# Per-tile reuse of the convolution's room, and constants made by GpSimd alone, in a convolution and attention hybrid

## The chip, the cores and the metric

The kernel runs on one core of a Trainium2 chip. A core has five engines with queues of their own: TensorE (PE in the profile, with PEld for its weight loads), VectorE (DVE), ScalarE (ACT), GpSimd (POOL) and SyncE (SP), which here only issues DMAs. Each takes its instructions in order. They meet through semaphores: an instruction can wait until a count that other instructions raise has reached a value. The metric is the device time of one execution in microseconds; lower is better. Before the change it is 2581.11 us, the median of five runs between 2576.23 and 2585.54.

## The reference

The input x has 128 images of 128 channels and 16x16 pixels. The model has two layers.

```
# layer 0
x = x + conv_block(group_norm(x))
#   conv_block: batch norm, 4-bit activations, 3x3 conv (4-bit weights, cross pattern),
#               batch norm, 4-bit activations, 3x3 conv (diagonal pattern), + its input
# layer 1, tokens t = pixels of x
t = t + mamba(ln(t), forward weights) + reversed mamba(ln(t), backward weights)
t = t + moe(ln(t))          # 8 experts, the best 2 of them, softmax of their scores
```

The batch norm of the convolution block has to see all images before any of them can go on, so layer 0 has three passes: statistics, the first convolution, the second convolution. Layer 1 treats each image by itself.

## The kernel before

Images are handled in 64 pairs. A pair is a tile of 128 channels by 512 pixels in float32, 256 KB, or 2 KB in each of the 128 partitions of the on-chip memory.

**Statistics and first convolution.** All 64 pairs of x are loaded into tiles xr0 to xr63 (lines 374 to 378), which stay on chip to the end of the second convolution. They live in the pool `res` with the second convolution's weights `wq2`, four padded images `hpad` and small tensors. The first convolution writes its output to DRAM (o1), apart from five pairs kept on chip.

**Second convolution** (`conv2`, lines 546 to 601). For each pair: the first convolution's output comes back from DRAM (q), ScalarE applies batch norm and Relu (L562), VectorE quantises into a padded image (L195), TensorE convolves (L222), GpSimd and at times ScalarE scale xr in place (L592, L590), VectorE adds (L593), TensorE transposes the result to tokens (L571), ScalarE copies it out of PSUM (L573), and SP stores it to DRAM as y (L574). GpSimd's scaling depends on little, so it runs far ahead of the other engines. Which taps and how many passes the convolution needs is decided on the chip: `by_weights` reads a flag and branches to one of three versions of the phase, so the code of the second convolution stands three times in the program, inside If blocks.

**The room.** When the convolution is done, `ress.close()` and `kepts.close()` release its pools, and the pools of the loop take over the same memory: `late` (constants), `pr` and `sm` (working tiles), `ps` (PSUM). A pool that lands on released pools waits, as written, for every user of those pools. So the first instruction that writes into `late` waits for the last use of anything in `res`.

**Constants** (`constants`, lines 619 to 639, with the memsets of line 646). `rows` and `cols` are three sets each of bf16 operands, 4 KB per partition, for a matmul that makes the decay matrices (part s, L933). A set of rows is filled by one ScalarE copy (a column repeated along the free axis, L623) and overwritten in its first 64 partitions by a VectorE copy of repeated identities (L624); a set of cols by a VectorE copy (L628) and eight GpSimd masks (L635). `gts`, `daz`, `lwz` and `far` are set by GpSimd memsets (L646, L620).

**The loop.** Layer 1 is written as small generators, the parts: a (load a pair of tokens, layer norm, transpose), c (time steps and decays, once per two pairs), x, z, s, y and so on, to f (experts and output). A part yields after each step. The table `T` gives every step a time, with 375 units for each two pairs; all steps of all pairs are sorted by it and issued in that order under `manual_schedule`, so it is the order on each engine. Part a of pair 0 has its steps at 60 (load yt0 from y, L712), 68 (statistics on VectorE, L693 to L696), 103 (the power -1/2 and two products on GpSimd, L699 to L701), 165 (normalize on ScalarE, L704), 270 (transpose on TensorE, L718) and 336 (copy from PSUM, L721); pair 1 has them at 191, 257, 313, 327, 385 and 395. Part c of these two pairs follows from 420 with the matmuls dt_ps (L734), which need both. `constants()` is called just before the steps. All DMAs before the change are issued by SP.

Of the kernel before, what the change touches and what calls it, by code (L numbers as in the profile page):

```python
# [8 lines left out]
F32 = mybir.dt.float32  # L9
# [5 lines left out]
P = 128  # L15
NT = 256
# [6 lines left out]
NH = 4  # L23
HD = 64
# [10 lines left out]
def kernel(ctx: ExitStack, tc: tile.TileContext, a: dict):  # L35

    nc = tc.nc
    x_d, out_d = a["x"], a["out"]
    B = x_d.shape[0]
    NP = B // 2  # L40
    NG = B // G
    PSUM = bass.MemoryType.PSUM

    x_c = x_d.rearrange("b c s -> c b s")
# [6 lines left out]
    y_d = [dram.tile([P, 4, P], F32, name=f"y_{i}", tag=f"y_{i}") for i in range(NP)]  # L51
# [8 lines left out]
    ident = const.tile([P, P], F32, name="ident")  # L60
# [32 lines left out]
    heads = const.tile([P, NH], F32, name="heads")  # L93
    triple = const.tile([P, 2], F32, name="triple")
# [166 lines left out]

    ress = ExitStack()
    res = ress.enter_context(tc.tile_pool(name="res", bufs=1))
    wq2 = res.tile([P, 9, 3, P], BF16, name="wq2")

    hpads = [res.tile([P, 2, 18, 18], F32, name=f"hpad{k}") for k in range(4)]
# [81 lines left out]
    with tc.tile_pool(name="w1p", bufs=1) as w1p:  # L348
# [15 lines left out]
        with tc.tile_pool(name="setup1", bufs=1) as setup, tc.tile_pool(  # L364
            name="psa", bufs=1, space=PSUM
# [5 lines left out]
                next(weights)  # L371


            xr = []
            for i in range(NP):
                t = res.tile([P, 2, NT], F32, name=f"xr{i}", tag=f"xr{i}")
                nc.sync.dma_start(t, x_c[:, 2 * i : 2 * i + 2, :])
                xr.append(t)
            load_weights()
            w2 = w1p.tile([P, 9, P], F32, name="w2", tag="w")  # L380
            nc.sync.dma_start(w2, a["L0_conv_w2"])
# [223 lines left out]
    ress.close()  # L605
    kepts.close()

    late = ctx.enter_context(tc.tile_pool(name="late", bufs=1))

# [7 lines left out]
    def constants():  # L619
        nc.gpsimd.memset(far, -1e30)  # L620
        for k in range(3):
            r, c = rows[k], cols[k]
            nc.scalar.copy(r.rearrange("p h d t l -> p h (d t l)"), heads.unsqueeze(2).to_broadcast([P, NH, 4 * P]))  # L623
            nc.vector.tensor_copy(  # L624
                r[0:HD].rearrange("p h d t (f l) -> p (h d t f) l", l=HD),
                ident[0:HD, 0:HD].unsqueeze(1).to_broadcast([HD, 2 * NH * 2 * 2, HD]),
            )
            nc.vector.tensor_copy(  # L628
                c.rearrange("p m d j f l -> p m (d j f l)"), triple.unsqueeze(2).to_broadcast([P, 2, 8 * P])
            )  # L630
            for d in range(2):
                for half in range(2):
                    sign = 1 - 2 * d
                    for m in range(2):
                        nc.gpsimd.affine_select(  # L635
                            out=c[0:HD, m, d, :, half, :], in_=far.unsqueeze(2).to_broadcast([HD, 2, P]),
                            pattern=[[0, 2], [sign, P]], compare_op=ALU.is_ge, fill=0.0,
                            base=-sign * HD * half - 1, channel_multiplier=-sign,
                        )
# [4 lines left out]
    lwz = late.tile([P, P], F32, name="lwz")  # L644
    for t in (*gts, daz, lwz):
        nc.gpsimd.memset(t, 0.0)  # L646
    pr = ctx.enter_context(tc.tile_pool(name="pr", bufs=2))
    sm = ctx.enter_context(tc.tile_pool(name="sm", bufs=2))
    ps_ = ctx.enter_context(tc.tile_pool(name="ps", bufs=1, space=PSUM))
    BANKS = {"x": 2, "y": 2, "o": 4}  # L650
    E0 = 5

# [3 lines left out]
    def bank4(name, tag):  # L656
        return bank(name, tag).rearrange("p (t l) -> p t l", l=P)
# [29 lines left out]
    def layernorm(src, dst, nm):  # L687

        s6 = sm.tile([P, 4, 6], F32, name=f"s6{nm}", tag="s6")
        mv = sm.tile([P, 4, 2], F32, name=f"mv{nm}", tag="mv")  # L690
        rstd = sm.tile([P, 4], F32, name=f"rstd{nm}", tag="rstd")
        for t in range(4):
            nc.vector.bn_stats(s6[:, t, :], src[:, t, :])  # L693
        for t in range(4):
            nc.vector.bn_aggr(mv[:, t, :], s6[:, t, :])
        alone(nc.vector.tensor_scalar(rstd, mv[:, :, 1], EPS, None, ALU.add))  # L696
        yield
        nmr = sm.tile([P, 4], F32, name=f"nmr{nm}", tag="nmr")
        nc.gpsimd.tensor_tensor(rstd, rstd, mhalf[:, :4], ALU.pow)  # L699
        nc.gpsimd.tensor_tensor(nmr, mv[:, :, 0], rstd, ALU.mult)  # L700
        nc.gpsimd.tensor_scalar(nmr, nmr, -1.0, None, ALU.mult)  # L701
        yield
        for t in range(4):
            nc.scalar.activation(  # L704
                dst[:, t, :], src[:, t, :], AF.Identity, bias=nmr[:, t : t + 1], scale=rstd[:, t : t + 1]
            )
        yield

    def part_a(i):

        yt = yts[i] = pr.tile([P, 4, P], F32, name=f"yt{i}", tag="yt", bufs=6)
        nc.sync.dma_start(yt, y_d[i])  # L712
        yield
        u = pr.tile([P, 4, P], F32, name=f"u{i}", tag="u", bufs=2)
        yield from layernorm(yt, u, f"a{i}")
        u_ps = bank4(f"u_ps{i}", "o")
        for t in range(4):
            nc.tensor.transpose(u_ps[:, t, :], u[:, t, :], ident)  # L718
        yield
        uT = uTs[i] = pr.tile([P, 4 * P], F32, name=f"uT{i}", tag="uT", bufs=4)  # L720
        nc.scalar.copy(uT, u_ps.rearrange("p t l -> p (t l)"))  # L721
        yield
# [425 lines left out]
    def part_f(i):  # L1148
# [83 lines left out]
    }  # L1232
    parts = {
        "a": part_a, "c": part_c, "x": part_x, "bc": part_bc, "sx": part_sx, "z": part_z, "xt": part_xt, "g": part_g,
        "s": part_s, "b": part_b, "m": part_m, "y": part_y, "n": part_n, "r": part_r, "o": part_o, "e": part_e, "p": part_p,
        "f": part_f,
    }
    steps = []
    for i in range(NP):
        for (name, *which), places in T.items():  # L1240
# [3 lines left out]
            steps += [(i // 2 * PERIOD + t, len(steps) + n, stream) for n, t in enumerate(places[i % 2])]  # L1244
    steps.sort(key=lambda step: step[:2])
    constants()
    with tc.manual_schedule():
        for _, _, stream in steps:
# [31 lines left out]
```

## Time and profile before

| | |
|---|---|
| median of five runs | 2581.11 us |
| the profiled execution | 2579.19 us, span 2577.5 us |
| PE, DVE, ACT, POOL busy | 94%, 88%, 85%, 64% of the span |
| second convolution on TensorE | about 175 to 294 us |
| the loop's first TensorE instruction | 312.12 us |
| steady part of the loop | about 420 to 2500 us |

The profile is one execution on the chip. Times are counted from the start of its span; the execution's own time holds 1.7 us more than the span. A line such as "L592 POOL TENSOR_SCALAR xr<-xr,ares,bres 128x256" is a group of instructions: line of the kernel, engine, operation, output and inputs, and the shape of the output; what follows is busy time, the mean of one, and the idle time of the engine just before. In lists by time the first two columns are start and length, x24 means 24 instructions in a row, and square brackets give how long the engine had been idle and what released it. POOLq and SPq are the sequencers that issue and wait for these engines. For the stretches of time, columns are named where they are shown.

### The profile page before, as it was taken

What the parts mean: (1) busy time and instruction counts of PE and PEld (TensorE: products, weight loads), DVE (VectorE), ACT (ScalarE), POOL (GpSimd) and SP (SyncE); (2) the same over time, 40 slices, a digit from 0 to 9 for tenths busy, and PEclk for the clock granted to TensorE, in tenths of its full rate; (3) what the DMA queues carried; (4) which work ended last, traced back from release to release, by engine and by line L of the source; (5) the groups of instructions that cost most, each with busy time, mean ns of one, the idle gap of its engine ahead of it and who ended that gap; (6) DMA issues with size and microseconds to landing.
All of it is one profiled execution on the core that took longest, in us unless ns stands there. A gap on an engine that the chain in (4) does not pass through costs nothing.

```text
span 2577.5 us, 49413 instructions
## 1 busy us (share of the span) xinstructions
PE 2434.4 (94%) x15940; PEld 1483.2 (58%) x15940; DVE 2259.6 (88%) x6193; ACT 2192.6 (85%) x4482; POOL 1656.1 (64%) x1727
## 2 busy tenths in 40 slices
PE   0889679999999999999999999999999999999997
PEld 0335345666666666666666666666666666666663
DVE  8877589999999999999999999999999999999883
ACT  6777579898988889889888898998888898988881
POOL 1777315666667666666676666666666666666666
PEclk9999889999999999999999999999999999999998
DMA  9458423443444444444434444343434444443343
GB/s 284 147 199 280 165 62 90 125 123 118 130 119 118 123 131 131 121 121 123 125 112 123 128 130 119 120 127 122 119 119 131 131 123 118 126 125 114 109 126 104
DMA packets 303030, 339.03 MB, mean 132 GB/s; under 512 B 56865, under 2 KB 226849, under 8 KB 302753
## 3 DMA queue, kind: packets, MB, share of 16 engines
q1 hardware_dynamic: 302752, 335.68, 43.1%
q8 instruction: 132, 2.16, 0.3%
q14 instruction: 146, 1.19, 0.2%
HBM read 261.41 MB, written 57.41 MB: 124 GB/s over the span
## 4 chain that ended last, share of the span: by engine, by line
PE 90%; DVE 3%; DMA 3%; ACT 2%; POOL 1%; issue 1%; SPq 0%; POOLq 0%; DVEq 0%; ACTq 0%
PE f_ps L1157 17%; PE x_ps L845 13%; PE y_ps L980 9%; PE z_ps L888 9%; PE o_ps L1040 9%; PE cv L222 5%; PE sg L933 5%; PE xt_ps L900 4%; PE y_ps L986 4%; PE g_ps L919 4%; DMA xr<-in_x 2%; PE n_ps L1013 1%; PE u_ps L718 1%; PE f_ps L1152 1%; PE u_ps L1062 1%; PE yt_ps L571 1%
## 5 line engine op out<-in xcount | busy, mean ns | idle before, releaser
L1145 POOL TENSOR_TENSOR gb<-gb,u2T 128x512 f32<-128x512 f32 x512 | 641.6, 1278 | 121.5 <-PE y_ps L986 60.2
L863 DVE SCALAR_TENSOR_TENSOR xc<-x_ps,cw,xc 128x510 f32<-128x510 f32 (+2 forms) x768 | 571.2, 744 | 46.6 <-ACT xc L857 37.2
L996 POOL TENSOR_TENSOR yg<-yg,z 128x512 f32<-128x512 f32 x256 | 325.8, 1278 | 352.2 <-DVE yg L992 155.4
L1157 PE MATMUL f_ps<-gb,ew 128*128 128x512 f32 x1024 | 511.7, 604 | 6.0 <-POOL gb L1145 5.8
L845 PE MATMUL x_ps<-uT,wx 128*128 128x512 f32 x768 | 401.9, 605 | 8.5 <-DVE xc L863 3.5
L673 ACT ACTIVATE e<-sg 128x512 f32<-128x512 f32 x512 | 299.5, 591 | 49.9 <-PE sg L933 44.5
L673 ACT ACTIVATE e<-e,ends 128x128 f32<-128x128 f32 x1024 | 325.0, 392 | 0.0
L980 PE MATMUL y_ps<-e,xt 128*64 128x256 f32 x2048 | 317.7, 389 | 0.2 <-DVE yg L992 0.2
L961 DVE TENSOR_TENSOR e<-e,g_ps 128x1024 f32<-128x1024 f32 x256 | 311.4, 1216 | 6.3 <-ACT e L673 2.6
L863 DVE SCALAR_TENSOR_TENSOR bc<-x_ps,cw,bc 128x510 f32<-128x510 f32 (+2 forms) x384 | 286.5, 746 | 20.5 <-ACT bc L857 5.2
L1157 PEld LDWEIGHTS f_ps<-gb,ew 128*128 128x128 f32 x1024 | 181.3, 192 | 173.6 <-issue 137.6
L888 PE MATMUL z_ps<-uT,wz 128*128 128x512 f32 x512 | 271.2, 611 | 2.0 <-DVE xc L863 1.4
L857 ACT ACTIVATE xc<-x_ps,cb,cw 128x512 f32<-128x512 f32 x256 | 199.1, 778 | 64.5 <-PE x_ps L845 57.9
L1040 PE MATMUL o_ps<-wo,yg 128*128 128x128 f32 x2048 | 251.0, 276 | 0.2 <-DVE e L966 0.2
L1040 PEld LDWEIGHTS o_ps<-wo,yg 128*128 128x128 f32 x2048 | 240.3, 193 | 11.1 <-DVE g L1117 8.4
L992 DVE SCALAR_TENSOR_TENSOR yg<-xc,dcol,y_ps 128x512 f32<-128x512 f32 x256 | 189.6, 741 | 50.4 <-PE y_ps L986 46.9
L1028 POOL TENSOR_TENSOR rr<-rr,mhalf 128x8 f32<-128x8 f32 x64 | 109.9, 1717 | 161.4 <-DVE g L1119 82.4
L986 PE MATMUL y_ps<-e,xt 128*64 128x128 f32 x2048 | 198.9, 273 | 0.0
L933 PE MATMUL sg<-rows,cols 128*128 128x256 bf16 x1024 | 192.2, 275 | 5.8 <-ACT e L673 2.8
L222 PE MATMUL cv<-hpad,wq 128*128 128x512 bf16 x640 | 179.1, 423 | 18.0 <-DVE hpad L195 8.8
L986 PEld LDWEIGHTS y_ps<-e,xt 128*64 128x64 f32 x2048 | 146.9, 137 | 74.2 <-DVE e L966 0.5
L980 PEld LDWEIGHTS y_ps<-e,xt 128*64 128x64 f32 x2048 | 118.8, 136 | 101.0 <-issue 53.9
(257 smaller groups left out, 4870.2 us busy)
## 6 DMA issues: line engine op xcount, KB each, us to landing
gb<-gd SPq DMA_DIRECT2D x256, 512.0 KB
e<-cum SPq DMA_DIRECT2D x256, 256.0 KB
xr<-in_x SPq DMA_DIRECT2D x64, 256.0 KB
y<-yt SPq DMA_DIRECT2D x64, 256.0 KB
yt<-y SPq DMA_DIRECT2D x64, 256.0 KB
cc<-bc SPq DMA_DIRECT2D x128, 128.0 KB
out<-ob SPq DMA_DIRECT2D x64, 256.0 KB
o<-o SPq DMA_DIRECT2D x59, 256.0 KB
```

The costliest lines, as they stand in the source:

```text
L673: nc.scalar.activation(out, in_, func, **more)
L845: nc.tensor.matmul(ps, wx[d][:, n * P : (n + 1) * P], uTs[i], start=True, stop=True)
L863: nc.vector.scalar_tensor_tensor(acc[:, :, to], raw[:, :, of], cw[:, d, n, 3 - back : 4 - back], acc[:, :, to], ALU.mult, ALU.add,)
L888: nc.tensor.matmul(ps, wz[:, d, n * P : (n + 1) * P], uTs[i], start=True, stop=True)
L933: nc.tensor.matmul(sg[:, :, of], c_[:, k, d, s, half, :], r_[:, :, d, s, of], start=True, stop=True)
L961: nc.vector.tensor_tensor(e0.rearrange("p h t l -> p h (t l)"), e0.rearrange("p h t l -> p h (t l)"), gps[i, d, k][:, 0:NT].unsqueeze(1).t ...
L980: nc.tensor.matmul(y_ps[64 * q : 64 * q + 64, k, :], xt[:, 2 * k + s0, 64 * h : 64 * h + 64], e0[:, h].rearrange("p t l -> p (t l)"), star ...
L986: nc.tensor.matmul(y_ps[64 * q : 64 * q + 64, k, s1 * P : (s1 + 1) * P], xt[:, 2 * k + s1, 64 * h : 64 * h + 64], e1[:, h, :], start=False ...
L996: large(nc.gpsimd.tensor_tensor(yg, yg, zs[i, d][:, n, :], ALU.mult))
L1040: nc.tensor.matmul(o_ps[:, (2 * j + d) * P : (2 * j + d + 1) * P], ygs[i, d, n][:, t * P : (t + 1) * P], wo[d][:, n, :], start=(n == 0), s ...
L1145: large(nc.gpsimd.tensor_tensor(gb[:, e], gb[:, e], u2Ts[i], ALU.mult))
L1157: nc.tensor.matmul(f_ps, ew[:, e, :], gbs[i, e], start=False, stop=(e == NE - 1))
```

## The change

Four edits go together.

- The tiles xr0 to xr63 are allocated first in `res`, so they lie at its beginning, where `late` and `pr` will come to lie.
- `late`, `pr`, `sm` and `ps` are opened with `reuse_waits="tile"`: each tile then waits only for the users of the earlier tiles that lay on its own bytes (in PSUM, its own bank).
- `rows` and `cols` are filled by GpSimd alone, in copies of 512 elements: per set four copies of a column of `heads`, four of repeated identities in 64 partitions, and four of a column of `triple`. The masks and memsets are as they were.
- The loads of yt0 and yt1 are issued from GpSimd's queue; those of all other pairs stay on SP.

```
     res = ress.enter_context(tc.tile_pool(name="res", bufs=1))
+    xr = [res.tile([P, 2, NT], F32, name=f"xr{i}", tag=f"xr{i}") for i in range(NP)]
     wq2 = res.tile([P, 9, 3, P], BF16, name="wq2")
...
-            xr = []
             for i in range(NP):
-                t = res.tile([P, 2, NT], F32, name=f"xr{i}", tag=f"xr{i}")
-                nc.sync.dma_start(t, x_c[:, 2 * i : 2 * i + 2, :])
-                xr.append(t)
+                nc.sync.dma_start(xr[i], x_c[:, 2 * i : 2 * i + 2, :])
...
-    late = ctx.enter_context(tc.tile_pool(name="late", bufs=1))
+    late = ctx.enter_context(tc.tile_pool(name="late", bufs=1, reuse_waits="tile"))
...
-            nc.scalar.copy(r.rearrange("p h d t l -> p h (d t l)"), heads.unsqueeze(2).to_broadcast([P, NH, 4 * P]))
-            nc.vector.tensor_copy(
-                r[0:HD].rearrange("p h d t (f l) -> p (h d t f) l", l=HD),
-                ident[0:HD, 0:HD].unsqueeze(1).to_broadcast([HD, 2 * NH * 2 * 2, HD]),
-            )
-            nc.vector.tensor_copy(
-                c.rearrange("p m d j f l -> p m (d j f l)"), triple.unsqueeze(2).to_broadcast([P, 2, 8 * P])
-            )
+            for h in range(NH):
+                nc.gpsimd.tensor_copy(
+                    r[:, h].rearrange("p d t l -> p (d t l)"), heads[:, h : h + 1].to_broadcast([P, 4 * P])
+                )
+                nc.gpsimd.tensor_copy(
+                    r[0:HD, h].rearrange("p d t (f l) -> p (d t f) l", l=HD),
+                    ident[0:HD, 0:HD].unsqueeze(1).to_broadcast([HD, 2 * 2 * 2, HD]),
+                )
+            for m in range(2):
+                for d in range(2):
+                    nc.gpsimd.tensor_copy(
+                        c[:, m, d].rearrange("p j f l -> p (j f l)"), triple[:, m : m + 1].to_broadcast([P, 4 * P])
+                    )
...
-    pr = ctx.enter_context(tc.tile_pool(name="pr", bufs=2))
-    sm = ctx.enter_context(tc.tile_pool(name="sm", bufs=2))
-    ps_ = ctx.enter_context(tc.tile_pool(name="ps", bufs=1, space=PSUM))
+    pr = ctx.enter_context(tc.tile_pool(name="pr", bufs=2, reuse_waits="tile"))
+    sm = ctx.enter_context(tc.tile_pool(name="sm", bufs=2, reuse_waits="tile"))
+    ps_ = ctx.enter_context(tc.tile_pool(name="ps", bufs=1, space=PSUM, reuse_waits="tile"))
...
         yt = yts[i] = pr.tile([P, 4, P], F32, name=f"yt{i}", tag="yt", bufs=6)
-        nc.sync.dma_start(yt, y_d[i])
+        (nc.gpsimd if i < 2 else nc.sync).dma_start(yt, y_d[i])
```

## The prediction

> **What bounds the kernel now.** I read the page's busy shares first, then the busy time by stage, then the waits between 290 and 420 us, and last the instructions in order of time around 294 us. TensorE is busy for 94% of the span, so only a stretch where it rests can give much. The busy time by stage (columns: stretch and length, then busy us and instructions of PE, PEld, DVE, ACT, POOL, then granted clock, DMA share, GB/s) shows one such stretch between the second convolution and the loop:
>
> ```profile
> 275.00:295.00 20.00, 18.32 (x96) 9.82 (x94) 11.46 (x19) 11.46 (x19) 0.88 (x1) 1.00 0.61 218
> 295.00:312.00 17.00, 0.00 (x0) 0.00 (x0) 10.29 (x32) 5.49 (x5) 16.75 (x33) 0.60 0.24 78
> 312.00:325.00 13.00, 9.92 (x42) 5.40 (x43) 6.00 (x25) 8.66 (x21) 2.44 (x6) 0.63 0.00 1
> 500.00:600.00 100.00, 100.00 (x678) 63.08 (x677) 91.02 (x255) 89.06 (x184) 66.76 (x64) 1.00 0.40 123
> ```
>
> From 295 to 312 us TensorE does nothing, and GpSimd is busy for 16.75 of 17 us. The waits of that part name the chain (waiter, releaser, us):
>
> ```profile
> POOL gt L646 <- PE yt_ps L571: 50.5, 1, 50.5
> PE u_ps L718 <- ACT u L704: 18.1, 1, 18.1
> ACT u L704 <- POOL nmra L701: 11.5, 1, 11.5
> ```
>
> GpSimd stands for 50.5 us until the last transpose of the convolution, then works; ScalarE waits for it, TensorE for ScalarE. In order of time (start, length), what the three others do:
>
> ```profile
> 294.05 2.45 DVE L628 CAST cols<-triple 128x2048 bf16<-128x2048 f32 x2 [0.81 <-PE yt_ps L571]
> 294.12 2.52 POOL L646 MEMSET gt<- 128x128 f32 x2 [50.48 <-PE yt_ps L571]
> 294.59 5.48 ACT L623 CAST rows<-heads 128x2048 bf16<-128x2048 f32 x3
> ...
> 300.40 9.53 POOL L635 TENSOR_SCALAR_AFFINE_SELECT cols<-far 64x256 bf16<-64x256 bf16 x24
> 301.34 0.86 DVE L693 BATCH_NORM_STATS2 s6a<-yt 128x6 f32<-128x128 f32 x4
> ...
> 309.90 1.03 POOL L699 TENSOR_TENSOR rstda<-rstda,mhalf 128x4 f32<-128x4 f32 x1
> ```
>
> The first layer norm is ready for its power (L699) at 302.8, but that sits behind 24 masks until 309.90. The anchor I follow is the second half of the first dt_ps group (L734), at 316.04 in the chain: everything in the loop hangs on it, and the loop is TensorE alone (100.00 of 100 us), so what the anchor moves, the end moves.
>
> **The change part by part.**
>
> *Constants leave ScalarE and VectorE.* Three casts of 5.48 us and six of 2.45 + 1.22 + 1.41 + 2.42 = 7.50 us go. Alone this is worth nothing, because GpSimd's 309.90 ends later than either.
>
> *They go to GpSimd.* Per set four heads copies and four identity copies (512 elements each) and four triple copies (512): 12, times 3 sets is 36; with them 24 masks and five memsets. No GpSimd copy is in the trace. The nearest row that reads one input and writes one output is the mask: 291 ns for 128x128 (L68) against 185 for 128x4 (L100), so 0.86 ns an element on a floor of 0.18. 512 elements make 0.62 us, which I take as 0.64. The other end is the scaling row, which ran beside VectorE:
>
> ```profile
> L592 POOL TENSOR_SCALAR xr<-xr,ares,bres 128x256 f32<-128x256 f32 x112 | 67.7, 619 | 0.0
> L506 POOL TENSOR_SCALAR q<-q 128x256 f32<-128x256 f32 x38 | 38.5, 1012 | 3.3
> ```
>
> Twice 0.59 (63.00 us for 107 of it between 180 and 243) is 1.18; twice 1.01 is 2.02 and the far end. Alone on the engine: 36 x 0.64 = 23.0, masks 24 x 0.40 = 9.5, memsets at the row of the start (0.20 for 128x128, L65) 0.9, and 2 for waits between dependent instructions: 35.4 us.
>
> *Beside VectorE they take longer.* The memset that took 0.20 at the start took 1.29 at 294 (L646) while VectorE cast without a pause: the two exclude each other for whole instructions. In the convolution VectorE's L195 (0.42 us, once per 1.72 us) does this. The Trainium skill, page "SBUF — State Buffer", section "Who interferes with whom", says the same as an exclusive lock in VectorE's two-port modes, and speaks against giving GpSimd more work here. Full exclusion makes a factor of up to 1/(1 - 0.42/1.72) = 1.32; I take 1.25, so 44.3 us. In return L195 grew from 0.41 (4.86 us for 12) to 0.57 (6.81 for 12) beside GpSimd; with L593 (0.75) VectorE is at 1.32 of 1.72, so the convolution's pace hides it.
>
> *When they start.* GpSimd's last scaling ends at 243.64. Its sequencer was through the branch and at the loop's first wait by 236.2:
>
> ```profile
> L646 POOLq EVENT_SEMAPHORE  x4: 43/388/56587, 236.2 to 293.3; - x4
> ```
>
> so no barrier closes the branch; only that wait of 56.6 us holds it. With xr first in its pool, the late tiles (six of 4 KB, then 2.5 KB) lie on xr0 to xr13, 2 KB each. xr13's transposes are over near 204, so the wait is gone. Constants end at 243.6 + 44.3 = 287.9; between 276 (mask rate, no exclusion) and 302 (1.18 a copy).
>
> *The loads of yt0 and yt1 move from SP to GpSimd.* yt0 lies on xr13 and xr14, free by 206. On SP it would stand behind the last store (294.7); SP loses two issues of 0.37 us, and yt2 goes out at 295.1 instead of about 297.6. No row shows a GpSimd DMA. The nearest is SP's load of the same 256 KB: the last fetch issued at 278.11, used at 282.15, 4.04 us; the two before took 3.57 and 4.47. I take 4.5 from issue to data, between 3.6 and the 6.0 of one xr load in the full queue. (The page "DMA: Bandwidth & Descriptors", section "Latency and other measured facts", gives about 1 us to the first byte from GpSimd and 0.6 from SP; by that the sum has 4.4 each.) So yt0 is there at 292.4, before VectorE's last add of the convolution ends (292.48 + 0.75). Slack: 0.9 us.
>
> *yt1 is issued behind the first power.* In the order of the steps GpSimd has yt0's DMA (60), power and two products of image pair 0 (103), then yt1's DMA (191). The second load therefore waits for VectorE's statistics of the first, and behind it stands only pair 1's own power.
>
> *The sum.* VectorE free 293.3; statistics 1.35 (0.86 + 0.35 + 0.17, which overlap a little); power and products 1.65 plus 0.05; yt1 lands 4.5 later; statistics 1.35; power and products 1.70; four normalizations 1.64 (half of 3.25); transposes, copy, first half of dt_ps 1.21 (314.83 to 316.04). 293.3 + 13.4 = 306.7. Against 316.04 that is 9.3 us less. The span goes from 2577.5 to 2568.2. The profiled execution's own 2579.19 us lies 1.9 below the median 2581.11; taken from the median, 2571.8 us. What is late next: yt1's load, where before it was the masks.
>
> *Per-tile waits in the loop's other pools* add some wait instructions on first use; 17 to 43 ns each on GpSimd's sequencer (L699's row of six). With some 20 on a chain, below 1 us; 0 taken, since most name releasers already passed. *TensorE's clock* was 0.60 to 0.81 from 295 to 345; a shorter rest may keep it higher. The x_ps pairs at 324 and 332 (1.91, 2.06 us) run 1.10 at full clock, so at most 3 us; 0 taken.
>
> **The rivals.**
>
> *B, the copies are slow enough to be the new bound.* Each us after 288.8 at which the constants end is one us of gain lost. At 1.18 us a copy they end at 302, the anchor at 319.9, the time 2585; at 0.80 the gain is about 3. For it: the scaling row; against: that row contains the exclusion already, without which it would be near 0.45 (0.59/1.32), close to the mask's rate for 256 elements, 0.40.
>
> *C, copies at the rate of L506.* 2.02 x 36 + 16 = 89 us, end at 332, time 2615. L504, same shape, does not show that rate.
>
> *D, slower: the tile waits are not followed through the branches.* Then GpSimd's first memset still waits for 294.05, but now has 35.4 us of work with nobody's help and yt0's load behind it: constants end at 329.5, anchor 329.5 + 4.5 + 13.4 = 347.4, 31 us later, 2612. It takes the whole gain once the constants end past 298.1, that is once that first wait lies past about 257, and decides for slower some six us later. Against it: the releaser is a semaphore count that TensorE passes at every image, and the sequencer already reached the wait without a barrier.
>
> *E, a load from GpSimd takes far longer than SP's.* With 9 us each the anchor is at about 315 (2580), with 12 at 321 (2586).
>
> **How the numbers follow.** Forecast (constants end by about 290) 0.60, B 0.13, C 0.06, D 0.10, E 0.11. Predicted 2572. The forecast's own range is 2564 to 2576: 9.3 us plus 3 for the clock and 5 for the scatter of runs (2576.23 to 2581.11), up to 4 less if loads take 6.0 and the constants end at 290. The range 2563 to 2594 takes B and E in and leaves C and D, 0.16, out. A difference of 0.2% is 5.2 us, about what a measurement can tell. Faster by more: the forecast and 0.03 of B, 0.63; within: the rest of B, half of E, 0.15; slower: C, D and the rest of E, 0.22.
>
> **What would show it.** Right: GpSimd busy from 243.7 to about 288 with copies near 0.8 us; no wait on L571 at the first memset; DVE L693 at 293.3; a second wait of VectorE for yt1's DMA near 300; dt_ps near 307; the loop from there as before. Wrong: constants past 290, copies over 1 us, the memset still at 294, or a load over 6 us.

## The result, and the profile after

The changed kernel takes 2580.67 us (median of 35 runs, 2575.22 to 2595.99); beside it the kernel before took 2579.1 us (59 runs, 2573.95 to 2585.54). The ratio is 1.0012, 95% interval 1.0005 to 1.0019: no difference that counts, where 9.3 us less were predicted. The 35 times are in two heaps, 27 between 2575.2 and 2584.2 and 8 between 2588.7 and 2596.0; before has one heap. The execution that was profiled is of the upper one: 2591.87 us, span 2590.2.

So two things have to be explained: where the gain went, and why the times scatter. The busy time by stage of the kernel after (columns as before: stretch and length, PE, PEld, DVE, ACT, POOL, granted clock, DMA share, GB/s):

```profile
243.00:250.00 7.00, 3.75 (x20) 1.82 (x18) 6.56 (x2) 3.27 (x5) 7.00 (x17) 1.00 0.57 188
250.00:275.00 25.00, 7.38 (x30) 3.72 (x30) 23.93 (x27) 3.89 (x7) 24.24 (x51) 0.65 0.22 74
275.00:295.00 20.00, 19.09 (x89) 11.10 (x90) 11.96 (x24) 12.46 (x20) 0.00 (x0) 0.84 0.81 258
295.00:312.00 17.00, 17.00 (x91) 9.44 (x90) 10.53 (x19) 10.22 (x17) 0.00 (x0) 1.00 0.70 239
312.00:325.00 13.00, 6.23 (x31) 3.36 (x29) 5.41 (x25) 4.04 (x8) 2.65 (x5) 0.77 0.47 161
```

The same view of the kernel before, for the second of these stretches:

```profile
250.00:275.00 25.00, 25.00 (x133) 14.03 (x132) 17.44 (x51) 17.98 (x29) 0.00 (x0) 1.00 0.90 289
```

The hole after the convolution is there no more: from 295 to 312 us TensorE works through. But a new one is in the middle of the convolution. From 250 to 275 us TensorE is busy for 7.38 us where it was busy for 25.00, while GpSimd is busy for 24.24 with the constants. VectorE looks busier than before (23.93 against 17.44 us) and does half as many instructions (27 against 51). Busy with so few means that single instructions take very long. In order of time:

```profile
243.21 0.34 POOL L649 MEMSET gt<- 128x128 f32 x2
...
243.94 1.17 POOL L622 CAST rows<-heads 128x512 bf16<-128x512 f32 x2
244.10 16.53 DVE L195 TENSOR_SCALAR hpad<-q 128x512 f32<-128x512 f32 x1
...
250.67 2.93 POOL L638 TENSOR_SCALAR_AFFINE_SELECT cols<-far 64x256 bf16<-64x256 bf16 x8
...
258.02 2.29 POOL L631 CAST cols<-triple 128x512 bf16<-128x512 f32 x4
260.26 3.66 POOL L638 TENSOR_SCALAR_AFFINE_SELECT cols<-far 64x256 bf16<-64x256 bf16 x8
260.56 0.74 DVE L591 SCALAR_TENSOR_TENSOR xr<-cv,less,xr 128x512 f32<-128x512 f32 x1
...
261.44 1.09 PE L569 MATMUL yt_ps<-ident,xr 128*128 128x128 f32 x4 [14.69 <-DVE xr L591]
...
265.40 6.34 DVE L341 COPY dtb<-few_dt_bias 128x8 f32<-128x8 f32 x4
...
273.46 0.78 POOL L715 DMA_DIRECT2D yt<-y  x1
...
275.90 1.09 PE L569 MATMUL yt_ps<-ident,xr 128*128 128x128 f32 x4 [7.08 <-DVE xr L591]
```

One quantisation (L195) that takes 0.41 us alone is on record for 16.53 us. It begins 0.16 us after GpSimd's first copy and is over only at the first mask of the second set, 32 GpSimd copies and masks later, all of them back to back. TensorE stands for 14.69 us behind it. Later four copies of 128x8 (L341 fills small tensors that the loop needs) take 6.34 us, and TensorE stands for 7.08 more. GpSimd's copies meanwhile are not slowed. Groups of GpSimd between 243 and 274 us (busy us, mean ns of one, idle):

```profile
L638 POOL TENSOR_SCALAR_AFFINE_SELECT cols<-far 64x256 bf16<-64x256 bf16 x24 | 9.5, 433 | 0.0
...
L622 POOL CAST rows<-heads 128x512 bf16<-128x512 f32 x12 | 7.0, 608 | 0.0
```

The convolution's last add (L591) ends at 316.39 us instead of 293.23. What follows it is as hoped:

```profile
315.64 0.75 DVE L591 SCALAR_TENSOR_TENSOR xr<-cv,less,xr 128x512 f32<-128x512 f32 x1 [0.96 <-PE cv L222]
...
316.31 0.86 DVE L696 BATCH_NORM_STATS2 s6a<-yt 128x6 f32<-128x128 f32 x4
...
317.74 1.05 POOL L702 TENSOR_TENSOR rstda<-rstda,mhalf 128x4 f32<-128x4 f32 x1 [43.50 <-DVE rstda L699]
...
319.65 0.63 POOL L715 DMA_DIRECT2D yt<-y  x1 [0.23 <-issue]
...
323.03 0.87 DVE L696 BATCH_NORM_STATS2 s6a<-yt 128x6 f32<-128x128 f32 x4 [5.38 <-DMA yt<-y]
...
329.01 0.20 PEld L737 LDWEIGHTS dt_ps<-uT,wdt 128*32 128x32 f32 x8 [0.48 <-ACT uT L724]
```

yt0 is there before VectorE is free, GpSimd has been idle for 43.5 us when the first power (L702, L699 before) comes, VectorE waits for yt1, and the second dt_ps begins 12.6 us after the last add, where it was 22.8. So the sum of this execution is: 23.2 us lost inside the convolution, 10.2 won behind it, 13.0 later at the anchor (329.01 against 316.03), and 12.7 in the span.

### The profile page after: what moved, and what is told of

Its sections match the earlier page's. It is cut to its first block, busy times and chain, and to the rows that moved or that the text cites. A ratio compares the mean times of both kernels' runs of the same rounds, so it can differ in the third digit from the quotient of the medians.

```text
span 2590.2 us, 49445 instructions
## 1 busy us (share of the span) xinstructions
PE 2440.6 (94%) x15940; PEld 1485.4 (57%) x15940; DVE 2275.2 (88%) x6187; ACT 2188.2 (84%) x4479; POOL 1675.1 (65%) x1765
## 4 chain that ended last, share of the span: by engine, by line
PE 89%; DVE 4%; DMA 3%; ACT 2%; issue 2%; POOL 1%; SPq 0%; POOLq 0%; DVEq 0%; ACTq 0%
PE f_ps L1160 17%; PE x_ps L848 13%; PE y_ps L983 9%; PE z_ps L891 9%; PE o_ps L1043 9%; PE sg L936 5%; PE cv L222 4%; PE xt_ps L903 4%; PE y_ps L989 4%; PE g_ps L922 4%; DMA xr<-in_x 2%; PE n_ps L1016 1%; PE u_ps L721 1%; PE f_ps L1155 1%; PE u_ps L1065 1%
## 5 line engine op out<-in xcount | busy, mean ns | idle before, releaser
L866 DVE SCALAR_TENSOR_TENSOR bc<-x_ps,cw,bc 128x510 f32<-128x510 f32 (+2 forms) x384 | 286.5, 746 | 20.9 <-ACT bc L860 4.5
L1043 PEld LDWEIGHTS o_ps<-wo,yg 128*128 128x128 f32 x2048 | 239.1, 192 | 11.1 <-DVE g L1120 8.4
```

Of the source, the lines that this page charges most:

```text
L866: nc.vector.scalar_tensor_tensor(acc[:, :, to], raw[:, :, of], cw[:, d, n, 3 - back : 4 - back], acc[:, :, to], ALU.mult, ALU.add,)
L1043: nc.tensor.matmul(o_ps[:, (2 * j + d) * P : (2 * j + d + 1) * P], ygs[i, d, n][:, t * P : (t + 1) * P], wo[d][:, n, :], start=(n == 0), s ...
```

## The experiments

**S**, the theory formed from this profile: GpSimd's instructions that follow each other without a gap hold a path into the on-chip memory that VectorE's plain copies and scalings from SBUF to SBUF need too (L195, L341, L343). Such a VectorE instruction does not surely get in between two GpSimd instructions, but can wait through many of them. The add L591, which reads PSUM, is not touched: it takes 0.75 us throughout. The first rival is that something else in the change made L195 slow, above all the new places of the tiles in memory; the second that the loads from GpSimd's queue or the other prices of the prediction ate the gain.

All versions in one table, each from its profiled execution. "End" is the end of the convolution's last add, "anchor" the start of the second half of dt_ps, "behind" the difference; from the anchor to the end of the span it is between 2259.7 and 2264.1 us in all fourteen, so what moves the anchor moves the end, within these 4.4 us. "Ratio" is to the kernel before on the same chip, with its 95% interval.

| version | median us | ratio | end | anchor | behind |
|---|---|---|---|---|---|
| before | 2579.1 | | 293.2 | 316.0 | 22.8 |
| after | 2580.67 | 1.0012 (1.0005–1.0019) | 316.4 | 329.0 | 12.6 |
| e1, after again | 2583.22 | 1.0027 (1.0008–1.0046) | 308.0 | 320.6 | 12.5 |
| e2, L195 reads PSUM | 2583.77 | 1.0018 (1.0008–1.0027) | 307.3 | 319.8 | 12.6 |
| e3, reuse alone | 2576.51 | 0.999 (0.9981–1.0) | 292.9 | 313.8 | 20.9 |
| e4, copies as scalings | 2585.13 | 1.0023 (1.0002–1.0043) | 300.3 | 313.0 | 12.7 |
| e5, L195 from PSUM, small copies moved | 2564.67 | 0.9942 (0.9926–0.9959) | 287.3 | 300.0 | 12.8 |
| e6, before with e5's two edits | 2575.84 | 0.9979 (0.997–0.9989) | 288.4 | 311.2 | 22.8 |
| e7, pauses | 2570.33 | 0.9963 (0.9949–0.9977) | 294.5 | 307.2 | 12.8 |
| e8, pauses, yt1 early | 2567.54 | 0.9947 (0.9931–0.9964) | 298.2 | 305.7 | 7.5 |
| e9, small copies moved | 2579.25 | 1.0 (0.9982–1.0017) | 310.4 | 323.2 | 12.7 |
| e10, e5 with loads on SP | 2563.59 | 0.9945 (0.9928–0.9961) | 287.1 | 299.5 | 12.4 |
| e11, e5 with yt1 early | 2559.58 | 0.9925 (0.9909–0.9942) | 290.6 | 298.2 | 7.6 |
| e12, e8 with small copies moved | 2563.83 | 0.9936 (0.992–0.9953) | 292.6 | 300.2 | 7.6 |

### e1: the changed kernel once more

No edit: does the starvation come in every execution, and in the same place?

> The changed kernel once more. Theory S (starved VectorE): the quantisation L195 reads and writes on-chip memory in a fast mode that needs the port GpSimd uses, and it cannot start while GpSimd's copies follow one another without a pause. Then some L195 or L341 between 243 and 274 us lasts several us again, though not the same ones for the same time; the second convolution ends some 9 to 22 us after 294, and from its end to the second dt_ps group it is 13.5 us again. Time 2575 to 2592. Rival P (placement): the new places of hpad and xr slow L195 whatever GpSimd does; then L195 is slow outside 243 to 274 as well, and by the same amount as in the first profile of this kernel.

2583.22 us over seven runs, from 2576.62 to 2592.5. Its profile, VectorE between 243 and 275 us:

```profile
248.31 2.50 DVE L195 TENSOR_SCALAR hpad<-q 128x512 f32<-128x512 f32 x1
...
254.94 2.31 DVE L343 TENSOR_SCALAR wo<-wo,nw 128x128 f32<-128x128 f32 x2
257.17 3.45 DVE L341 COPY dtb<-few_dt_bias 128x8 f32<-128x8 f32 x4
...
263.61 1.09 PE L569 MATMUL yt_ps<-ident,xr 128*128 128x128 f32 x4 [7.61 <-DVE xr L591]
```

The same three lines of VectorE are held, in the same stretch, but for other lengths: there no L195 takes more than 2.50 us, where one took 16.53, and the convolution ends 8 us sooner than in the first profile. This execution is of the lower heap, the first one of the upper, and their times differ by 8.7 us; so the difference arose inside the convolution, where these waits are. What decides how long one of them lasts is not shown; where VectorE's instruction happens to fall in GpSimd's series is the likely answer. Against the kernel before the convolution still ends 14.8 us later here. TensorE rests for 8.25 us of that between 250 and 275 us, at a granted clock of 0.80; the rest was not taken apart. Outside the stretch L195 is as in the kernel before, which speaks against the tiles' new places, since they would act all through the convolution.

### e2: L195 reads PSUM

```
-                nc.scalar.activation(q, q, AF.Relu, bias=bi2, scale=sc2)
-                quantise(q, hpads[i % 4], nq)
+                if nq == 1:
+                    qp = psw.tile([P, 2, NT], F32, name=f"qp{i}", tag="qp", bufs=2)
+                    nc.scalar.activation(qp, q, AF.Relu, bias=bi2, scale=sc2)
+                    quantise(qp, hpads[i % 4], nq)
...
```

ScalarE leaves its result in PSUM, so L195 has the source that L591 has.

> ScalarE's batch norm and Relu of the second convolution writes to PSUM, and L195 reads from there, so that it has one operand on GpSimd's side only. GpSimd's constants stay as in the changed kernel. S: no L195 over 1.2 us, the second convolution ends at 294 to 296, its end to the second dt_ps group 13.5 us, time 9 us under the kernel before, 2570. L341's small copies still can be starved, which would leave some us. P: as the changed kernel, 2579 to 2592.

2583.77 us (2582.05 to 2587.39). L195 is held no more, each takes 0.68 us. But the small copies still read SBUF:

```profile
246.97 9.14 DVE L341 COPY dtb<-few_dt_bias 128x8 f32<-128x8 f32 x4
256.02 5.79 DVE L341 COPY aneg<-few_A_log 128x8 f32<-128x8 f32 x4
261.73 3.62 DVE L343 TENSOR_SCALAR wo<-wo,nw 128x128 f32<-128x128 f32 x2
...
267.62 1.09 PE L574 MATMUL yt_ps<-ident,xr 128*128 128x128 f32 x4 [16.97 <-DVE xr L596]
```

Ten instructions take 18.55 us; the same ones took 0.16 to 0.28 each in the kernel before. TensorE rests for 16.97 us behind them. They end with GpSimd's series, at 265. S had 2570 us here and named the small copies as what could be left; they took the whole gain. The source of the operation decides whether it is held, and its size does not: one copy of 128x8 is on record for 5.20 us, and L195 with its 128x512 from PSUM for 0.68.

### e3: the reuse by tiles alone

The tiles xr first and the four pools with per-tile waits, as in the change; constants on ScalarE, VectorE and GpSimd, and all loads on SP, as before.

> One part alone: xr first and per-tile waits, but the constants' copies on ScalarE and VectorE and all loads on SP, as before. S: the second convolution ends at 294, no slow L195; GpSimd's memsets are over by 244, its masks run from about 295.5 to 305.5, so the first power starts near 305.5 where it started at 309.9; time 4 us less, 2575. P: the second convolution is late by 9 to 22 us here too, time 2585 to 2597.

2576.51 us, 2.1 less than before beside it and at the edge of what can be told, where 4 less were expected. The wait for the convolution's end is gone, and GpSimd sets its memsets at once; the casts of the constants by ScalarE and VectorE stand at the end of their queues, and the masks behind them:

```profile
243.43 1.47 DVE L195 TENSOR_SCALAR hpad<-q 128x512 f32<-128x512 f32 x1
243.87 0.35 POOL L644 MEMSET gt<- 128x128 f32 x2
...
294.21 13.47 POOL L633 TENSOR_SCALAR_AFFINE_SELECT cols<-far 64x256 bf16<-64x256 bf16 x24 [49.27 <-DVE cols L626]
```

13.47 us for 24 masks that took 9.53: here VectorE's casts were first, and GpSimd was the one that waited. The first line is the large effect in small: one L195 of 1.47 us over the five memsets. And the first rival is out: the tiles have their new places here, and the convolution ends at 292.9 us, no later than before. The reuse alone is thus worth some 2 us; most of what is to be had needs the constants out of the way.

### e4: GpSimd's copies as scalings

```
-                nc.gpsimd.tensor_copy(
-                    r[:, h].rearrange("p d t l -> p (d t l)"), heads[:, h : h + 1].to_broadcast([P, 4 * P])
+                nc.gpsimd.tensor_scalar(
+                    r[:, h].rearrange("p d t l -> p (d t l)"), ones[:, 0:1].to_broadcast([P, 4 * P]),
+                    heads[:, h : h + 1], lwz[:, 0:1], ALU.mult, ALU.add,
                 )
```

and the same for the identities and the triples. In both kernels GpSimd's scaling of xr (L592, L590) runs back to back for 43 us and more, and L195 beside it only grows from 0.42 to 0.59 us. So perhaps the copy is the culprit and not the missing gap.

> GpSimd's 36 copies are made by the two-operation scaling with per-partition scalars (times a column, plus zero), the form of the scaling that ran beside the second convolution without holding VectorE up. If what starves VectorE is that copies leave no gap and scalings do: L195 at most 1.2 us, convolution ends at 294 to 295; each piece about 1.05 us, the constants end at 243 + 36 x 1.05 + 12 = 293, anchor near 311, time 2576. If any row of back-to-back GpSimd work with 512 elements starves it: L195 of many us again, the convolution ends 20 to 40 us late, time 2590 to 2610.

2585.13 us, five runs in two heaps (2575.51 and 2576.13; 2585.13 to 2589.18). In the profiled one, of the lower heap, L195 is at most 0.94 us, the small copies take up to 2.58 us for four (TensorE rests for 5.51 us behind them), and GpSimd's pieces take 0.83 to 0.89 us on average instead of 0.61. So in this execution scalings let VectorE in sooner than copies did in e1, also of a lower heap. But three of the five runs are in the upper heap, none of them was profiled, and the 2576 us that went with "copies leave no gap and scalings do" came in two runs of five. Whether scalings are the better form, and why, is left open.

### e5 and e6: nothing in the stretch that can be held

e5 is e2 with the step of the small copies moved 16 image pairs later, behind GpSimd's series:

```
-                if i % max(NP // 8, 1) == max(NP // 8, 1) - 1:
+                if i % max(NP // 8, 1) == max(NP // 8, 1) - 1 and i not in (39, 47):
```

> The quantisation reads PSUM as in the run before it of that name, and the step of the second convolution that makes 20 small VectorE copies and scalings (L340 to L342), which fell into GpSimd's constants, comes 16 image pairs later, when GpSimd is through. Theory S (VectorE's two-port operations starve while GpSimd works without a pause): nothing is left to starve, the second convolution ends at 294 to 295, the second dt_ps group is 13.5 to 14 us later, time 8 to 9 us less than the kernel before, 2570. If VectorE is held up by something else in the convolution, some VectorE instruction between 236 and 275 still takes over 2 us and the time stays near 2579 to 2584.

e6 makes these two edits in the kernel before, to separate what they are worth by themselves.

> The control: the same two edits (quantisation from PSUM, small copies 16 pairs later) in the kernel before. S: the convolution keeps its 1.72 us per pair, GpSimd has no constants in it, so the time is that of the kernel before within 2 us, 2579. If these edits themselves help, it is faster, and the gain of the run with both is not the change's.

e5 takes 2564.67 us, ratio 0.9942. In its profile, beside GpSimd's unbroken series:

```profile
249.45 0.68 DVE L195 TENSOR_SCALAR hpad<-qp 128x512 f32<-128x512 f32 x1
250.02 2.28 POOL L636 CAST cols<-triple 128x512 bf16<-128x512 f32 x4
...
250.50 0.75 DVE L596 SCALAR_TENSOR_TENSOR xr<-cv,less,xr 128x512 f32<-128x512 f32 x1 [0.37 <-PE cv L222]
251.17 0.68 DVE L195 TENSOR_SCALAR hpad<-qp 128x512 f32<-128x512 f32 x1
```

L195 takes 0.68 us each time, more than the 0.42 of the source in SBUF, and keeps the convolution's beat of 1.72 us. TensorE is busy for 25.00 of 25 us from 250 to 275. e6 takes 2575.84 us, 4.3 less than before, which was to be within 2: beside GpSimd's scalings, too, the source in PSUM helps (TensorE is busy for 67.95 us of the 68 from 175 to 243, and for 64.11 in the kernel before). What the change adds on top of the two edits is the difference of e5 and e6, taken in one session: 11.2 us less, and 11.1 less at the anchor (300.03 against 311.15). The 9.3 us that were predicted are in it in full. It also says most of why e5 came out 5 us under its 2570: the edits help by themselves.

### e7: a pause behind each GpSimd instruction

```
+    def paused(made, last=[]):
+        if last:
+            info = mybir.DependencyInfo(mybir.DependencyClass.Sync, mybir.DependencyReason.DATA)
+            tc.add_manual_dep(made.ins, last.pop().name, info, reason="pause")
+        last.append(made.ins)
...
-                nc.gpsimd.tensor_copy(
+                paused(nc.gpsimd.tensor_copy(
```

Each of the 60 copies and masks waits until the one before it is complete; work and VectorE's operations are those of the change. `constants()` is also called inside `manual_schedule` here; GpSimd's order in the profile is the same as in the change. This is the experiment between "GpSimd works beside VectorE" and "GpSimd works without a gap".

> The changed kernel, with each of GpSimd's 60 copies and masks waiting for the one before to be complete (order kept). S, if it is the lack of a pause that lets GpSimd keep the port: each wait leaves some 0.06 to 0.1 us, VectorE gets in between, L195 takes at most 1.3 us, the constants end near 243 + 60 x 0.65 + 13 = 290, the second convolution ends at 294 to 297, the anchor near 309, time 2571 to 2574. If a pause is not enough, L195 and L341 of many us stay, and the time is 2580 to 2592.

2570.33 us (2569.61 to 2574.75), ratio 0.9963, 9.8 us less than the kernel before beside it. The profile:

```profile
244.34 0.61 POOL L629 CAST rows<-heads 128x512 bf16<-128x512 f32 x1
244.71 0.52 DVE L195 TENSOR_SCALAR hpad<-q 128x512 f32<-128x512 f32 x1
245.01 0.68 POOL L632 CAST rows<-ident 64x512 bf16<-64x512 f32 x1
...
248.14 0.76 DVE L341 COPY dtb<-few_dt_bias 128x8 f32<-128x8 f32 x4
```

The gaps are some 0.07 us (4.0 us of idle time in 60), L195 takes 0.57 us on average, and no VectorE instruction in the stretch takes more than 1 us. The constants end at 281.3 us, and GpSimd still stands for 13.54 us before the first power asks for it. Pauses of 4 us in all bring back the gain that was forecast.

### e8: yt1's load ahead of the first power

e7 with the step of yt1's load at time 61 instead of 191, so that GpSimd issues it right behind yt0's:

```
-            steps += [(i // 2 * PERIOD + t, len(steps) + n, stream) for n, t in enumerate(places[i % 2])]
+            steps += [(i // 2 * PERIOD + t, len(steps) + n, stream) for n, t in enumerate(
+                [61, *places[1][1:]] if (name, i) == ("a", 1) else places[i % 2])]
```

> As the run with pauses, and yt1's load is issued right behind yt0's, ahead of the first power. Both loads are then there when the second convolution ends. The prediction named yt1's load as what is late next: then VectorE does both statistics in a row, and the second dt_ps group comes 4 to 5 us earlier against the end of the convolution: 9 instead of 13.5 us after it. Time 4 to 5 us under the run with pauses. If GpSimd's load is hidden anyway, no difference.

2567.54 us, 2.8 less than e7 by the medians, where 4 to 5 were expected, and with intervals that overlap. The profile is clearer than the times: the anchor comes 7.5 us behind the last add instead of 12.8. The profiled execution itself is no faster than e7's (2571.70 against 2570.94 us): its convolution's first add starts 2.1 us later and its last one ends 3.7 later, so the anchor is only 1.5 us sooner. The prediction had named this load as what would be late next, and it was.

### e9 to e12: which part, and the best version

e9 is the changed kernel with e5's move of the small copies alone, L195 still reading SBUF; e10 is e5 with the loads of yt0 and yt1 on SP; e11 is e5 with e8's edit; e12 is e8 with the move. They ran in one session.

> The changed kernel with the one step of small copies (L341, L343) moved 16 image pairs later, and L195 still reading SBUF. It asks whether the small copies or L195 carry the loss. If S holds, GpSimd's unbroken copies meet only L195 now, which waits through them: one or more L195 of over 2 us between 243 and 275, TensorE without work for some of that, and a time of 2570 to 2582, 5 us or more above the version in which L195 reads PSUM as well (2564.7). If the small copies alone were the cause, no L195 exceeds 1 us and the time is within 2 us of 2564.7.

2579.25 us, ratio 1.0: ten runs, five from 2568.0 to 2574.7 and five from 2583.81 to 2587.65. The profiled one is of the upper five:

```profile
242.55 16.31 DVE L195 TENSOR_SCALAR hpad<-q 128x512 f32<-128x512 f32 x1
...
258.50 3.65 POOL L638 TENSOR_SCALAR_AFFINE_SELECT cols<-far 64x256 bf16<-64x256 bf16 x8
258.78 0.74 DVE L591 SCALAR_TENSOR_TENSOR xr<-cv,less,xr 128x512 f32<-128x512 f32 x1
```

L195 is held again for 16.3 us, again into the masks of the second set, and a later one for 5.46. The middles of the two heaps are 13 us apart (2573.2 and 2586.0), about what TensorE loses in the long wait (14.47 us, and 3.52 behind the later one); no run of the lower heap was profiled, so that those have no such wait is only likely. So both, L195 and the small copies, carry the loss, and neither cure of one alone is enough (e2, e9). That GpSimd's unbroken series holds these operations is shown by e5 and e7 together; what the two engines share is not seen in any trace.

> The version with L195 reading PSUM and the small copies moved (2564.7), with the loads of yt0 and yt1 back on SyncE. It prices the move of the loads alone. By the prediction, yt0 then stands behind the last store and arrives some 4 us after the convolution's end, but yt1 follows it at once instead of behind the first power: the second dt_ps group 10 to 14 us after the convolution's end, against 13.5 to 14 with the loads on GpSimd, so the time is between 2561 and 2566. A rival in which the move of the loads is worth several us gives 2568 or more.

2563.59 us, ratio 0.9945, against e5's 0.9942 with the loads on GpSimd on another chip: the same. Its anchor comes 12.4 us behind the last add, e5's 12.8. The second load behind the first power costs what the first load behind the last store costs.

> L195 reading PSUM, the small copies moved, and the load of yt1 issued ahead of the first power. All the losses that the runs have named so far are out: the second dt_ps group about 8.5 to 10 us after the convolution's end instead of 13.5, 3 to 5 us less than 2564.7, so 2560 to 2562. If the load is not on the path here, within 1 us of 2564.7.

2559.58 us, ratio 0.9925, 4.0 less than e10 beside it and 18.7 less than the kernel before. The anchor is 7.6 us behind the last add. Among these versions the move of the loads to GpSimd is worth something only with this order. This version beats both kernels and has the lowest time of the study.

> GpSimd's pauses, the small copies moved, and yt1's load ahead of the first power, with L195 still reading SBUF. If pauses alone let VectorE in, moving the small copies adds nothing: within 1.5 us of 2567.5, the version without the move. If the small copies still cost waits in spite of the pauses, or the moved place is better in itself, 2562 to 2565.

2563.83 us, ratio 0.9936 against e8's 0.9947. The intervals overlap, so whether the move still helps where there are pauses stays open; in the profiles one of the small operations takes 0.19 to 0.35 us on average in the new place and 0.20 to 0.35 in e8's, the old one, which shows no gain.

## Why the prediction was wrong

- **The step that failed** is "Beside VectorE they take longer". It saw that the two engines exclude each other and put the price on GpSimd: a factor of 1.25 on its work, and L195 at 0.57 us, hidden by the convolution's pace. Measured, GpSimd was not slowed (a copy 0.61 us, constants from 243.2 to 273.5 us, 30.3 us against 44.3 predicted), and VectorE paid: 16.53 us for one L195, 21.8 us of rest on TensorE in the profiled run (14.69 and 7.08). The two rows it rested on, the memset of 1.29 us beside VectorE's casts and the L195 of 0.57 us beside the scalings, were both read rightly, and both were cases in which neither engine locked the other out for more than one instruction. GpSimd's side of the exclusion got bounds (276 and 302 us for the end of the constants), VectorE's side none, although VectorE feeds TensorE and has only 0.40 us of slack in 1.72. And the trace before has a row that gives the other direction, which the prediction did not look for, since it lies in the first convolution. In order of time:

```profile
144.99 2.37 POOL L183 TENSOR_TENSOR w<-t_c,wq 128x1152 f32<-128x1152 f32 x1
145.29 2.35 DVE L195 TENSOR_SCALAR hpad<-q 128x512 f32<-128x512 f32 x1
...
147.70 1.43 PE L222 MATMUL cv<-hpad,wq 128*128 128x512 bf16 x5 [0.57 <-DVE hpad L195]
```

  One L195 of 2.35 us under one GpSimd product of 2.37. Looking up the longest L195 of the trace beside its mean would have shown that it can wait for GpSimd to the end of an instruction. That it waits through a whole series no row of before shows.
- The page of the Trainium skill "SBUF — State Buffer", section "Who interferes with whom", was weighed there as a price for GpSimd. It also says that the order of issue decides who waits, and that the other one is blocked for the whole instruction; in this change GpSimd's series was first. The runs here agree on who waits, but the wait is not one instruction of 0.61 us: it went through 32 of them.
- **The range**: 2580.67 us lies inside the wide range of 2563 to 2594, but by luck. That range was made to take in B and E, and neither came; the forecast's own range ended at 2576. None of the four signs of being wrong came either (constants past 290, copies over 1 us, the memset still at 294, a load over 6 us): they all watched GpSimd, and none watched the convolution.
- **Constants at 0.64 us a copy**: right, 0.61. The sum of 35.4 us alone was 5 too long: the copies follow each other every 0.56 us, which makes 20.2 us of 36 and not 23.0, and the 2 us for waits between instructions did not come, for there were no waits, which is the trouble.
- **When they start**: right. The first memset (243.21) follows the last scaling and waits for no transpose of the convolution's end. Rival D is out.
- **yt0 hidden**: right; the statistics start as soon as VectorE is free. **yt1 behind the first power, 4.5 us**: mis-sized, 3.36 us from issue to landing in the profiled run and 3.25 to 3.50 in others; the rest was right, and e8 and e11 show it as the late one (5.2 and 5.1 us from the last add to the anchor).
- **The sum from VectorE's last add to dt_ps**: 13.4 predicted, 12.5 to 12.8 measured in the seven profiles that have the change's order of loads. In e7, where the convolution ends at 294.5, the anchor is at 307.2 and the time 2570.3, beside 306.7 and 2572 predicted. What was forecast is what the change does when VectorE is let in.
- **SP's loads**: the move was priced at nothing lost on the path and 0.9 us of slack; e10 shows that it was also nothing won.
- **The rivals**: B (slow copies), C (the rate of L506) and E (a slow load from GpSimd) are out by 0.61 and 3.36 us. None of them is what happened; the price lay in the running convolution and not behind it, where the forecast and all rivals looked for it.
- **The clock**: from 250 to 275 us, where TensorE rested, 0.65 was granted, against 1.00 in the kernel before, where it did not rest, and the transposes just after the rests took 1.09 us for four instead of 0.60. The prediction had put the clock's gain behind the convolution only.

## What to carry to other kernels

When work is moved onto GpSimd beside a running stage, price both directions: not only how much longer GpSimd takes, but what happens to every VectorE operation in that stretch that copies or scales from SBUF to SBUF, small ones included, if it has to wait for the end of GpSimd's series. Where VectorE feeds the bounding engine, break the series by a wait between GpSimd's instructions, let the VectorE operation read PSUM, or move it out of the stretch, and do so for every such operation: with only one of two kinds cured nothing was gained here (e2, e9). And a time that falls into two heaps after an edit can be a sign of such a wait, long in one execution and short in the next; one profile shows only one of the cases.

## What the runs showed of the hardware

- A VectorE scaling of 0.41 us was held for 16.53 and 16.31 us by GpSimd copies of 0.61 us each without a gap, and four copies of 128x8 for 9.14 us. With gaps of some 0.07 us between GpSimd's copies and masks (e7) none was held for more than 0.45 us. The five memsets, which got no gaps, held an L195 to 1.47 us in e3 and 1.44 in e12.
- The exclusion also works the other way: where VectorE's casts were there first (e3), GpSimd's 24 masks grew from 9.53 to 13.47 us. But none of them took longer than 1.38 us; no wait went through a series.
- GpSimd's scalings of 256 elements, also without a gap (71 in 43.67 us), hold L195 by 0.17 us on average. Scalings of 512 elements held the small copies for up to 2.58 us in four. What tells them from copies was not tested. One difference is in the traces: a copy of 0.61 us starts every 0.56 us, so it starts some 0.05 us before the one ahead of it ends, while the scalings of 256 elements (0.63 us on average, one every 0.615) and those of e4 start only some 0.015 us before. In e7 there is a gap in place of this overlap.
- L195 from PSUM takes 0.68 us where it takes 0.42 from SBUF, and yet the whole kernel is faster with it beside GpSimd (e6, ratio 0.9979).
- A load of 256 KB issued by GpSimd behind the convolution took 3.25 to 3.50 us from issue to landing, its issue 0.63 us of the engine. Beside the convolution the landing took 3.1 to 7.2 us (after and e11), the issue up to 0.78.
